# Layer 0's aggregation taken before its projection, its first loads in another order, and another order of the additions at the end of layer 1

## The chip, the cores and the metric

The kernel runs on one core of one Trainium2 chip. Its metric is the device time of one launch in microseconds. Five engines work side by side, each with an instruction queue of its own that is taken strictly in order: TensorE (PE, with its weight loads shown as PEld), VectorE (DVE), ScalarE (ACT), GpSimd (POOL) and the queue engine SyncE (SP). An instruction that waits holds back everything behind it on its engine, the DMAs that this engine issues among them.

## The reference, cut to what matters

There are 3327 tokens with 256 features, padded to 26 tiles of 128 tokens, and a dense adjacency of 3327 x 3327 numbers of which few are not zero. Each of two layers adds a graph aggregation and then a mixture of experts:

```python
# layer 0
x = x + relu(adj @ (layernorm(x) @ W) + b)
x = x + moe0(layernorm(x))                 # top 2 of 8 experts, hidden size 1024
# layer 1
x = x + relu(new_adj @ (tanh(layernorm(x) @ W_proj + b_proj) @ W_gcn) + b_gcn)
x = x + moe1(layernorm(x))                 # top 2 of 8 experts, hidden size 256
```

`new_adj` is tanh of the squared positive entries of `adj`, of which at most the 700 largest of each row are kept. No row has so many, so the kernel counts the positive entries and takes the branch without a selection.

## The kernel before, in words

The code is unrolled Python, and a scheduler fixes the order in each engine's queue when the kernel is built. Everything is 32-bit float; a matmul of 32-bit numbers is two records in the trace, and the counts of records below are those of the trace.

**Start of layer 0.** SP loads x tile by tile (L134), the weight W into `proj_sb` (L136), and then adjacency. The adjacency comes in 13 panels of 256 target nodes, each in two pieces of 13 source tiles (1664 KB each); a ring of six pieces in SBUF holds three panels. For each tile DVE computes the statistics (L267 to L279), PE turns the tile as it is, without normalising it (L305), ACT copies the result (L306), PE multiplies it by W (L313), and ACT writes the product, scaled by the tile's deviation, into `s` (L318). The mean is taken out of W itself once (L1053 to L1056). Ahead of all this 32 small matmuls on a constant keep PE busy (L144, `WARM`).

**Aggregation (`aggregate`, L345).** Both layers call it. For each panel the adjacency tile is the stationary operand and a tile of `s` the moving one, so that each of two PSUM sums holds 128 nodes by 256 features: 52 matmuls for a panel (L359). DVE adds bias, relu and x (`add_relu`, L323 and L324). Then `after0` routes the panel's two tiles: layernorm, 16 dot products with the gate (L379), the two best experts (`weights`, L436), an exponential on ACT (L444). One panel later `list_tokens` gives each token its row in an expert's list: four small matmuls on PE (L465, L466) and four scatters by POOL (L483). While this goes on ACT counts the positive entries of each piece with 16 sign activations a panel (`count`, L1069); a panel's piece of the ring is free when PE and ACT have both read it, and SP's load of the panel three further on waits for that (L341).

`after0(0)` also has SP turn two small gate weights through DRAM element by element (L1085), has POOL load the first of them onto all partitions (`load_gate`, L247), and has SP fill the first rows of all experts' lists (`fill`, L1035 and L1037, 32 DMAs).

**Experts (`experts`, L753).** The lists are worked in blocks of 256 tokens. A `step` loads blocks ahead, multiplies one (`first`, L873, activation L880), turns the next one (`turned`, L861 and L864) and multiplies on (`second`, L912); DVE adds the bias and scales (L919, L920), and POOL scatters the rows to DRAM (L483). After the first two steps of layer 0 the list of the last panel is made and the later blocks are planned.

**End of layer 1.** There are 32 steps, the last six of which work half blocks of 128 tokens. Beside the steps SP reads back the finished rows of pairs of tiles (`load_outputs`, L980), DVE adds them to x (`add_loaded`, L994), and ACT's queue stores the pair (L1329). In the branch that is taken a pair's additions come two steps after its read, inside the loop of steps. After the loop the last two pairs of tiles, which need every scatter, are read, added and stored (`finish`, L1287).

Of the kernel before, what the change touches and what calls it, by code (L numbers as in the profile page):

```python
# [10 lines left out]
F32 = mybir.dt.float32  # L11
# [11 lines left out]
P = 128  # L23
NT = 26
# [51 lines left out]


BEGUN, FIRST_TILES, MORE_TILES = 12, 14, 22
WARM = 32
TIERS = 3  # L80
# [10 lines left out]
def gnn_moe_two_layers(  # L91
# [38 lines left out]
    cum = state.tile([P, NT + 1, E], BF16, name="cum")  # L130

    proj_sb = const.tile([P, DC, D], F32, name="proj_sb")
    for t, n in [(0, 2)] + [(t, 4) for t in range(2, NT, 4)]:
        nc.sync.dma_start(out=x[:, t : t + n, :], in_=x_in[:, t : t + n, :])  # L134
        if t == 0:
            nc.sync.dma_start(out=proj_sb, in_=g0_w.rearrange("(c p) n -> p c n", p=P))  # L136


# [7 lines left out]
    make_identity(nc, ident)  # L146
    mean = ring[RING - 1][:, 0:P]
    nc.gpsimd.memset(mean, 1.0 / D)
    ones = const.tile([P, 1], F32, name="ones")
# [92 lines left out]

    f1_r_sb = by_feature("f1_r_sb", f1_rT)
    gates = []

    def load_gate(g):
# [4 lines left out]

    g1_bp_sb = plain("g1_bp_sb", g1_bp)
    f1_b1_sb = plain("f1_b1_sb", f1_b1)
    g1_wg_sb = by_feature("g1_wg_sb", g1_wg)

# [52 lines left out]

    def node_features(i, lhsT, w_sb, scale=None):

        ps = psy.tile([P, D], F32, name="ps_s", tag="py")
        for c in range(DC):
            nc.tensor.matmul(  # L313
                ps, lhsT=lhsT[:, c, :], rhs=w_sb[:, c, :], start=(c == 0), stop=(c == DC - 1)
            )
        if scale is None:
            return nc.scalar.copy(s[:, i, :], ps)
        return nc.scalar.activation(s[:, i, :], ps, AF.Copy, scale=scale)  # L318

# [10 lines left out]

    def piece(pan, k):
        return ring[(pan * NCHUNK + k) % RING].rearrange("p (c w) -> p c w", w=PW)

    last_piece, output_loads = [], []

    def load_panel(pan, prepare, earlier=()):

        for k in range(NCHUNK):
            a = piece(pan, k)
            with behind(earlier):  # L340
                d = nc.sync.dma_start(out=a, in_=adjT[pan, k])  # L341
            last_piece[:] = [d]
            prepare(pan, k, a)

    def aggregate(b_sb, prepare, after, loaded=0, count=None):  # L345

        for pan in range(NPAN):
# [3 lines left out]
            chunks = [piece(pan, k) for k in range(NCHUNK)]  # L351
            if count:
                count(pan, chunks)
            ps = [psy.tile([P, D], F32, name="ps_g", tag="py") for _ in range(PW // P)]
# [11 lines left out]
            for it in range(PW // P):  # L366
                add_relu(x[:, pan * (PW // P) + it, :], ps[it], b_sb)
            after(pan)

    def rows_of(a, t0, n):  # L370
# [382 lines left out]
    def experts(xlist, ys, group, fixed, n_hidden, func, w1T, b1, w2T, b2, copy, kept=None):  # L753
# [179 lines left out]

        def step(late, end=always, place=None):

            t = len(started)
            started.append(t)
            while len(loaded) < min(t + RING // places, end):
                load(late)
            if t not in ready:  # L940
                ready[t] = turned(loaded[t][1], groups_of(t))
            _, _, w1, bb1, _, _ = loaded[t]
            hT = first(ready.pop(t), w1, bb1, groups_of(t))
            if t + 1 < min(len(loaded), end):
                ready[t + 1] = turned(loaded[t + 1][1], groups_of(t + 1), place)
            second(t, late, hT)
# [68 lines left out]
    def fill(*lists):  # L1015


        with tc.issue_after(last_feature.ins):
            wide = blk.tile([P, H // P, SB], F32, name="wide").rearrange("p h b -> p (h b)")
# [12 lines left out]
            for xlist in lists:  # L1032
                for e in range(E):
                    first = xlist[e * NP : e * NP + SB, :].rearrange("(g p) d -> p g d", p=P)
                    nc.sync.dma_start(out=first[:, :, 0:ID], in_=zeros)  # L1035
                    with nc.allow_non_contiguous_dma("two elements of a partition"):
                        nc.sync.dma_start(  # L1037
                            out=first[:, :, ID : ID + 1], in_=rows_f[:, e, :].unsqueeze(2)
                        )

    deviation = {}
    for t0, n0 in [(0, 2), (2, 2), (4, 4), (8, 4), (12, 6), (18, 8)]:
        _, rs = statistics(t0, n0)
        deviation.update((t0 + g, rs[:, g : g + 1]) for g in range(n0))
        for t in range(t0, t0 + n0, 2):
            xT = turned_tiles([x[:, t + g, :] for g in range(2)])
            if t == 0:  # L1050
                ps = psy.tile([P, D], F32, name="ps_mean", tag="py")
                for c in range(DC):
                    nc.tensor.matmul(  # L1053
                        ps, lhsT=mean, rhs=proj_sb[:, c, :], start=(c == 0), stop=(c == DC - 1)
                    )
                nc.vector.tensor_tensor(  # L1056
                    proj_sb, proj_sb, ps.unsqueeze(1).to_broadcast([P, DC, D]), ALU.subtract
                )
            for g in range(2):
                last_feature = node_features(  # L1060
                    t + g, xT[:, :, ts(g, P)], proj_sb, deviation[t + g]
                )

    def count(pan, chunks):
        with tc.issue_after(last_feature.ins):
            for k, a in enumerate(chunks):
                for i in range(PW // GROUP):
                    sign = work.tile([P, CJ, GROUP], BF16, name="sign", bufs=1)
                    nc.scalar.activation(  # L1069
                        sign, a[:, :, ts(i, GROUP)], AF.Sign, bias=below,  # L1070
                        accum_out=positive[:, pan, i, k : k + 1],
                    )
# [6 lines left out]
    def after0(pan):  # L1079
        if pan == 0:  # L1080
            with tc.issue_after(last_piece[0].ins):
                for name, w in (("gate0", f0_wgT), ("gate1", f1_rT)):
                    g = dram.tile([E, D], F32, name=name)
                    with nc.allow_non_contiguous_dma("a few thousand elements"):
                        nc.sync.dma_start(out=g.rearrange("e d -> d e"), in_=w)  # L1085
                    gates.append(g)
            load_gate(gates[0])
            fill(xlist0, xlist1)
        if FREE_PAN <= pan < NPAN - 1:
            layer0.load(None)  # L1090
        t, n = PAIRS[pan]
        list_waiting()
        xn = layernorm(t, n)
# [6 lines left out]

    aggregate(gnn_b_sb, lambda pan, k, a: None, after0, count=count)

    layer0.step(None)
    layer0.step(None)
# [188 lines left out]
    with tc.If(first_usual > 0) as arms:  # L1293
# [28 lines left out]
        with tc.If(second_usual > 0) as inner:  # L1322
            layer1.know(2 * E)
            waiting, asked, added, k = [], [], [], 0
            while len(layer1.started) < layer1.always:
# [5 lines left out]
                if at == EARLY + 2 * E - 2:  # L1331
                    layer1.know_rest(late1)
                with behind(last_y):
                    if asked and at > asked[0][2] + 1:
                        yt, tiles, _ = asked.pop(0)
                        add_loaded(yt, *tiles)
                        added.append(tiles)
# [6 lines left out]
                if at in (EARLY + E, EARLY + 2 * E):  # L1344
                    tiles = range(0, FIRST_TILES, 2) if at == EARLY + E else range(FIRST_TILES, MORE_TILES, 2)
                    waiting.extend(((t, 2), at, list(outputs)) for t in tiles)
            assert not (waiting or asked)
            for tiles in added:
                nc.scalar.dma_start(out=rows_of(out, *tiles), in_=x[:, tiles[0] : sum(tiles), :])
            finish([(t, 2) for t in range(MORE_TILES, NT, 2)])  # L1350
        with inner.Else():
# [171 lines left out]
```

## Time and profile before

| What | Value |
|---|---|
| median of 3 runs | 1236.31 us (1234.97 to 1237.64) |
| the profiled execution's own time | 1235.14 us |
| its span | 1233.4 us, so 1.7 us lie around it |
| granted TensorE clock, mean | 0.99 |
| PE busy | 1198.3 us, 97% of the span |
| DVE, ACT, POOL busy | 698.1, 522.6, 271.7 us |
| DMA | 241.59 MB, mean 196 GB/s |

A line of the timeline gives the start in us, the length in us, the engine with the line of the kernel, the operation, what it writes and reads, how many instructions are merged in the line, and in brackets how long the engine had been idle and what released it. SPq, ACTq and POOLq are the parts of those engines that issue DMAs. Neighbouring lines of PE overlap a little, because matmuls are pipelined and their ends are modelled; distances between starts are what counts.

### The profile page before, as it was taken

How to read it: one execution, taken by the hardware profiler on the slowest of the kernel's cores; microseconds unless marked ns; L12 is line 12 of the kernel's file. 1: busy time of each engine (PE TensorE's matmuls, PEld its weight loads, DVE VectorE, ACT ScalarE, POOL GpSimd, SP SyncE). 2: the span in 40 equal slices, each digit the busy share in tenths (PEclk: the TensorE clock that was granted, in tenths of full speed). 3: DMA queues.
4: the chain of work that ended last, by engine and by line, in shares of the span. 5: the costliest groups of instructions: out<-in, count | busy, mean ns of one | idle time of the engine just before them, and what ended most of it. 6: DMA issues, size and time to landing. Idle time of an engine off the chain costs nothing. (4 is left out here: it accounts for less than half of the span.)

```text
span 1233.4 us, 18208 instructions
## 1 busy us (share of the span) xinstructions
PE 1198.3 (97%) x5853; PEld 1037.4 (84%) x5853; DVE 698.1 (57%) x2812; ACT 522.6 (42%) x963; POOL 271.7 (22%) x339
## 2 busy tenths in 40 slices
PE   8999999999999999999999999999999999999973
PEld 7888888888888888888888888888888888888862
DVE  6057877677664111211121167568999999786453
ACT  4869545541022222322222225896455453043331
POOL 2003131131231111111111110002323223255531
PEclk9999999999999999999999999999999999999996
DMA  9696455454167655766657657244445442477695
GB/s 349 187 241 246 176 201 176 147 191 142 63 233 231 208 195 175 240 201 204 233 179 229 224 223 268 79 167 172 164 177 195 161 158 90 128 245 248 209 288 195
DMA packets 122537, 241.59 MB, mean 196 GB/s; under 512 B 24352, under 2 KB 92992, under 8 KB 115392
## 3 DMA queue, kind: packets, MB, share of 16 engines
q1 hardware_dynamic: 107760, 205.33, 50.1%
q0 software_dynamic: 11136, 31.60, 7.0%
q10 hardware_dynamic: 3536, 3.41, 0.8%
q8 instruction: 48, 0.79, 0.3%
q14 instruction: 57, 0.47, 0.1%
HBM read 203.98 MB, written 36.33 MB: 195 GB/s over the span
## 5 line engine op out<-in xcount | busy, mean ns | idle before, releaser
L359 PE MATMUL ps_g<-s,ring 128*128 128x256 f32 x2704 | 588.2, 380 | 0.0
L359 PEld LDWEIGHTS ps_g<-s,ring 128*128 128x128 f32 x2704 | 512.0, 190 | 68.7
L873 PE MATMUL ps_h<-xT,ring 128*128 128x256 f32 (+1 forms) x1176 | 251.1, 366 | 3.3 <-ACT xT L864 2.1
L873 PEld LDWEIGHTS ps_h<-xT,ring 128*128 128x128 f32 x1176 | 205.6, 191 | 40.6 <-ACT wide L880 5.8
L880 ACT ACTIVATE wide<-ps_h,ring 128x256 f32<-128x256 f32 (+1 forms) x240 | 110.3, 460 | 283.9 <-PE ps_h L873 283.0
L379 DVE SCALAR_TENSOR_TENSOR rt_product<-xn,gate 128x256 f32<-128x256 f32 x400 | 198.0, 495 | 12.4
L912 PE MATMUL ps_y<-ring,wide 128*128 128x256 f32 x896 | 200.3, 379 | 0.0
L483 POOL DMA_INDIRECT xlist<-xn,rt_idx x104 | 106.4, 1023 | 398.6 <-DVE ln_ve L270 281.8
L912 PEld LDWEIGHTS ps_y<-ring,wide 128*128 128x128 f32 x896 | 167.1, 190 | 21.0
L1069 ACT ACTIVATE sign<-ring,below 128x416 bf16<-128x416 f32 x208 | 133.5, 642 | 66.4 <-DMA ring<-in_adjT 60.2
L483 POOL DMA_INDIRECT ys<-narrow,index x56 | 55.1, 985 | 330.9 <-DVE narrow L920 238.1
L1220 ACT ACTIVATE ring<-ring 128x3328 f32<-128x3328 f32 x22 | 65.4, 2979 | 87.2 <-DVE ring L1219 56.6
L864 DVE COPY xT<-ptb 128x512 f32<-128x512 f32 (+1 forms) x29 | 19.0, 654 | 147.0 <-PE ptb L861 147.0
L919 DVE TENSOR_TENSOR narrow<-ps_y,ring 128x256 f32<-128x256 f32 x56 | 23.8, 424 | 133.7 <-PE ps_y L912 130.7
L323 DVE TENSOR_TENSOR gnn_t<-ps_g,gnn_b_sb 128x256 f32<-128x256 f32 x52 | 21.9, 420 | 112.1 <-PE ps_g L359 99.0
L483 POOL DMA_INDIRECT ys<-wide,index x58 | 58.2, 1004 | 60.1 <-DVE wide L920 34.5
L1221 ACT ACTIVATE ring<-ring 128x3328 f32<-128x3328 f32 x22 | 65.4, 2977 | 0.6
L444 ACT ACTIVATE rt_d<-rt_d 128x2 f32<-128x2 f32 x26 | 5.3, 202 | 117.3 <-DVE rt_d L443 117.3
L912 PE MATMUL ps_y<-s,narrow 128*128 128x256 f32 (+1 forms) x200 | 49.3, 387 | 0.1
L267 DVE BATCH_NORM_STATS2 ln_st<-x 128x6 f32<-128x256 f32 x104 | 42.9, 419 | 4.0 <-DMA x<-in_x 2.9
L861 PE MATMUL ptb<-ident,ring 128*128 128x128 f32 x228 | 36.3, 279 | 5.3 <-ACT narrow L880 5.1
L1219 DVE TENSOR_SCALAR ring<-ring 128x3328 f32<-128x3328 f32 x22 | 41.3, 1883 | 0.0
(215 smaller groups left out, 964.2 us busy)
## 6 DMA issues: line engine op xcount, KB each, us to landing
ring<-in_adjT SPq DMA_DIRECT2D x52, 1664.0 KB, 7.6
ring<-in_f_w1T SPq DMA_DIRECT2D x30, 1024.0 KB, 6.2
ring<-in_f_w2T SPq DMA_DIRECT2D x30, 1024.0 KB, 8.1
ring<-xlist SPq DMA_DIRECT2D x52, 258.0 KB, 3.1
ring<-in_f_w SPq DMA_DIRECT2D x36, 256.0 KB, 3.6
ring<-ys SPq DMA_DIRECT2D x14, 512.0 KB, 4.2
ring<-in_f_b SPq DMA_DIRECT2D x34, 128.0 KB, 7.5
xlist<-wide SPq DMA_DIRECT2D x16, 257.0 KB, 6.3
```

What stands on the lines that cost most here:

```text
L267: nc.vector.bn_stats(out=st, in_=x[:, t0 + g, :])
L359: nc.tensor.matmul(ps[it], lhsT=chunks[k][:, c, ts(it, P)], rhs=s[:, j, :], start=(j == 0), stop=(j == NT - 1),)
L379: nc.vector.scalar_tensor_tensor(product, xn[:, g, 0, 0:D], 1.0, gate[:, e, :], ALU.mult, ALU.mult, accum_out=sc[:, g, e : e + 1],)
L483: d = nc.gpsimd.indirect_dma_start(out=a[:, :], out_offset=bass.IndirectOffsetOnAxis(ap=index, axis=0), in_=rows_, in_offset=None,)
L861: nc.tensor.transpose(pt[:, c, ts(g, P)], xb[:, g, ts(c, P)], ident)
L873: nc.tensor.matmul(ps, lhsT=w1[:, c, ts(hc, P)], rhs=xT[:, c, :], start=(c == 0), stop=(c == DC - 1),)
L880: nc.scalar.activation(hT[:, hc, :], ps, func, bias=bb1[:, hc : hc + 1])
L912: last_product[:] = [nc.tensor.matmul(ps, lhsT=hT[:, hc, ts(g, P)], rhs=w2[:, hc, :], start=(hc == 0), stop=(hc == hc_n - 1),)]
L1069: nc.scalar.activation(sign, a[:, :, ts(i, GROUP)], AF.Sign, bias=below, accum_out=positive[:, pan, i, k : k + 1],)
L1219: nc.vector.tensor_scalar(a, a, 0.0, None, ALU.max)
L1220: nc.scalar.activation(a, a, AF.Square)
L1221: nc.scalar.activation(a, a, AF.Tanh)
```

## The change

**Layer 0 aggregates the normalised tokens.** `aggregate_first` takes the place of `aggregate` in layer 0 (layer 1 keeps it). DVE writes the normalised tiles straight into `s`. A tile of `s` is the stationary operand now and the adjacency the moving one, so that a panel's two sums hold 128 features by 256 nodes: 52 matmuls as before. ACT copies the two sums out, and four matmuls a panel (`finish`, 8 records) multiply by W behind the panel: six source tiles into the next panel (`BEHIND`), and for the last panel inside the first step of the experts. The first two panels are worked source tile by source tile side by side for the first 13 tiles; after that each panel by itself. The turning of x, the copies of it and the product with the mean are gone. The constant matmuls ahead are 54 instead of 32.

**Loads.** x and the first pieces of panels 0 and 1 are loaded in five groups of tiles in turn, W after the second pieces of these panels. The first gate is turned ahead of panel 2's pieces, the second behind them. The lists are filled in two halves, at panels 1 and 4. Four small weights are loaded later. The list of panel 0 is made a panel later.

**End of layer 1.** In the last six steps no additions are made any more: four pairs of tiles wait until behind DVE's last output. The last four tiles are read, added and stored one by one, and two of these stores go by SP's queue.

```diff
-WARM = 32
+WARM = 54
+BEHIND = 5
...
-    for t, n in [(0, 2)] + [(t, 4) for t in range(2, NT, 4)]:
+    for t, n in [(0, 2), (2, 2), (4, 4), (8, CJ - 8), (CJ, NT - CJ)]:
         nc.sync.dma_start(out=x[:, t : t + n, :], in_=x_in[:, t : t + n, :])
-        if t == 0:
-            nc.sync.dma_start(out=proj_sb, in_=g0_w.rearrange("(c p) n -> p c n", p=P))
+        if t < CJ:
+            for pan in range(2):
+                nc.sync.dma_start(
+                    out=piece(pan, 0)[:, t : t + n, :], in_=adjT[pan, 0, :, t : t + n, :]
+                )
...
+    def aggregate_first(b_sb, w, w_sb, begin, count, after):
+        sums, waiting, copied = {}, [], []
+        def start(pan):
+            sums[pan] = [psy.tile([P, PW], F32, name="ps_g", tag="py") for _ in range(DC)]
+        def add(pan, j):
+            for c in range(DC):
+                nc.tensor.matmul(
+                    sums[pan][c], lhsT=s[:, j, ts(c, P)],
+                    rhs=piece(pan, j // CJ)[:, j % CJ, :],
+                    start=(j == 0), stop=(j == NT - 1),
+                )
+        def finish():
+            pan, g = waiting.pop()
+            for it in range(PW // P):
+                ps = psh.tile([P, D], F32, name="ps_o", tag="ph")
+                for c in range(DC):
+                    nc.tensor.matmul(
+                        ps, lhsT=g[:, c, ts(it, P)], rhs=w_sb[:, c, :], start=(c == 0),
+                        stop=(c == DC - 1),
+                    )
+                add_relu(x[:, pan * (PW // P) + it, :], ps, b_sb)
+            after(pan)
+        def rest(pan, first):
+            for j in range(first, NT):
+                add(pan, j)
+                if waiting and j == first + BEHIND:
+                    finish()
+            g = work.tile([P, DC, PW], F32, name="xnT", bufs=2)
+            for c in range(DC):
+                copied.append(nc.scalar.copy(g[:, c, :], sums[pan][c]))
+            waiting.append((pan, g))
+        loaded = RING // NCHUNK
+        for pan in range(loaded):
+            load_panel(pan, lambda pan, k, a: None, begun=1 if pan < 2 else 0)
+            if pan == 1:
+                nc.sync.dma_start(out=w_sb, in_=w.rearrange("(c p) n -> p c n", p=P))
+                with tc.issue_after(last_piece[0].ins):
+                    turn_gate(f0_wgT)
+        with tc.issue_after(last_piece[0].ins):
+            turn_gate(f1_rT)
...
+        for j in range(CJ):
+            for pan in range(2):
+                add(pan, j)
+        for pan in range(NPAN):
...
+            begin(pan)
+            count(pan, copied)
+            rest(pan, CJ if pan < 2 else 0)
+        return finish
...
     for t0, n0 in [(0, 2), (2, 2), (4, 4), (8, 4), (12, 6), (18, 8)]:
-        _, rs = statistics(t0, n0)
...
+        with behind(last_normalized if t0 < 12 else ()):
+            layernorm(t0, n0, xn=s[:, t0 : t0 + n0, :].unsqueeze(2))
...
-    aggregate(gnn_b_sb, lambda pan, k, a: None, after0, count=count)
-
-    layer0.step(None)
+    def begin(pan):
+        if pan in (1, 4):
+            fill(xlist0 if pan == 1 else xlist1)
+
+    finish_last = aggregate_first(gnn_b_sb, g0_w, proj_sb, begin, count, after0)
+
+    layer0.step(None, between=finish_last)
     layer0.step(None)
...
                 with behind(last_y):
-                    if asked and at > asked[0][2] + 1:
+                    if asked and asked[0][2] + 1 < at <= layer1.always - FIXED[1]:
                         yt, tiles, _ = asked.pop(0)
                         add_loaded(yt, *tiles)
                         added.append(tiles)
...
-            for tiles in added:
-                nc.scalar.dma_start(out=rows_of(out, *tiles), in_=x[:, tiles[0] : sum(tiles), :])
-            finish([(t, 2) for t in range(MORE_TILES, NT, 2)])
+            left = []
+            for i, t in enumerate(range(MORE_TILES, NT)):
+                yt = ring[i][:, 0 : K * D].rearrange("p (n d) -> p n d", n=1)
+                load_outputs(yt, ys1, t, 1, outputs)
+                left.append((yt, (t, 1)))
+            with behind(last_y):
+                for i, (yt, tiles) in enumerate([(yt, tiles) for yt, tiles, _ in asked] + left):
+                    add_loaded(yt, *tiles)
+                    queue = nc.sync if i > len(asked) and i % 2 else nc.scalar
+                    queue.dma_start(out=rows_of(out, *tiles), in_=x[:, tiles[0] : sum(tiles), :])
```

## The prediction

> **What bounds the kernel now.** I read the page first (PE busy 97% of the span, clock 0.99), then who waits on PE, then the timelines of the two places that the change touches. PE waits for others for some 14 us in all, so time is won by taking work off PE or by letting it start earlier, and behind PE's last matmul by shortening the end. PE's timeline at the start:
>
> ```profile
> 4.57 2.04 PE L1053 MATMUL ps_mean<-proj_sb,ring 128*128 128x256 f32 x4
> 14.76 3.72 PE L313 MATMUL ps_s<-proj_sb,xnT 128*128 128x256 f32 x16 [2.30 <-ACT xnT L306]
> ...
> 41.03 45.06 PE L359 MATMUL ps_g<-s,ring 128*128 128x256 f32 x208
> ```
>
> Aggregation begins at 41.03, behind the whole projection. From 41.03 to the next group at 85.92 are 208 records, so a record is 0.216 us, a matmul 0.43, a panel 22.5. At 335.41 the first step of the experts begins.
>
> DVE's timeline gives the price of a layernorm, at the start and in panel 0:
>
> ```profile
> 3.79 0.75 DVE L267 BATCH_NORM_STATS2 ln_st<-x 128x6 f32<-128x256 f32 x2 [2.62 <-DMA x<-in_x]
> ...
> 65.27 0.17 DVE L270 TENSOR_SCALAR ln_ve<-ln_mv 128x2 f32<-128x2 f32 x1
> ...
> 67.72 0.73 DVE L289 TENSOR_SCALAR xn<-x,ln_mv,ln_guess 128x256 f32<-128x256 f32 x2
> ```
>
> The chain of small operations between statistics and normalising takes 2.45 us (65.27 to 67.72) however many tiles share it, a tile's normalising 0.37.
>
> The DMA view of the first 60 us, GB/s in slices of 1.5 us:
>
> ```profile
> GB/s 0 162 255 246 360 345 144 357 403 419 431 431 419 408 426 426 426 426 426 426 426 426 426 426 435 365 119 1 0 1 1 4 12 23 24 94 135 239 310 351
> ```
>
> By 12 us 2.8 MB have come, then 0.42 MB a us. At the end, DVE's timeline and the chain that ended last:
>
> ```profile
> 1213.78 0.42 DVE L919 TENSOR_TENSOR wide<-ps_y,gate 128x256 f32<-128x256 f32 x1
> 1215.31 0.69 DVE L994 TENSOR_TENSOR x<-x,ring 128x512 f32<-128x512 f32 x1 [1.05 <-DMA ring<-ys]
> 1215.92 0.35 DVE L920 TENSOR_SCALAR wide<-wide,ring 128x256 f32<-128x256 f32 x1
> 1227.70 1.42 DVE L994 TENSOR_TENSOR x<-x,ring 128x512 f32<-128x512 f32 x2 [0.16 <-DMA ring<-ys]
> ```
>
> ```profile
> 1216.55 5.59 DMA ys<-wide,index
> ...
> 1223.12 4.50 DMA ring<-ys
> ```
>
> PE's last product ends near 1213.1, yet the last output is scaled only at 1215.92: an addition that waits 1.05 us for its read stands in between. The last scatter (1216.55), the last read and the additions follow one another.
>
> **Start, the gain.** PE's time before 41.03 disappears: projection, turning, its waits. In its place PE starts when two tiles are normalised: statistics at 3.79 as now, small operations from 4.80, normalising from 7.25, so the first matmul at 7.6 instead of 41.03. The 54 constant matmuls, at 3.6 us for 32 (L144), end near 7.2 and cost nothing.
>
> **Start, what PE still waits for.** A source tile feeds both panels with 8 records, 1.73 us. DVE works groups of 2, 2, 4, 4, 6 and 8 tiles, the first four strictly one after another: 0.37 + 0.15 a tile for statistics, 2.45 for the chain, then 0.37 a tile. So tile 2 is ready at 11.8, tile 4 at 16.8, tile 8 at 22.5; in the last two groups statistics and small operations interleave as they do now from 11 to 20 us, so tile 12 comes at 31 to 32.5. PE has used up two tiles at 11.1, four at 15.3, twelve at 30.6: it waits 0.7, 1.5 and 0.4 to 1.9, 2.6 to 4.1 in all. I take 3.4, bounds 2 (if DVE interleaves better) and 7 (each group 1 us later). The present wait of 2.30 at 14.76 left the clock at full, so none of these should cost clock.
>
> **Start, loads.** Each source tile brings 3 x 131 KB, and PE uses them at 227 GB/s. The first 13 tiles are 5.1 MB, here at 17.5 us by the curve above, and used until 32; the second pieces come at 26 to 30 and are needed at 34 and 46. DVE, not DMA, sets the pace, so I price the splitting at nothing; without that cover it costs whatever a piece is late. The row for small transfers: the first 256 KB of x landed in 3.0 us, with slices of 162 to 360 GB/s. The Trainium skill speaks against the split ("DMA: Bandwidth & Descriptors", table of measured bandwidth): batch to 1 MiB or more for three quarters of the peak, and at 64 KB about a third. By a third of 420 GB/s the 5.1 MB would take 36 us and PE would lose some 7 more; the slices of this trace are already above that rate, and I stay with them.
>
> **Panels.** 52 matmuls of the same shape as before, with the operands' roles exchanged: 22.5 us, unchanged. Added on PE: 8 records a panel, 13 x 1.73 = 22.4 us. These are the 104 records of L313 moved, no longer at the start but behind each panel. Start in sum: 41.03 - 7.6 - 3.4 - 22.4 = 7.6 us gained, bounds 4.0 and 9.0.
>
> **What hides the rest.** ACT copies two sums a panel (0.47 each by L318) behind 16 signs (0.77 apart, 12.3 us of a panel of 24.3). The built order of ACT puts the exponential of panel p-1 ahead of panel p's copies, so routing must not lag: DVE's chain from bias to exponential takes 15.0 (63.67 to 78.70) to 16.9 us with a list in it, starts 6 us into the next panel, and is over at 23 of 24.3. The PE queue needs the copies only 5.2 us into the panel after; 5 us of cover. Behind that wait would stand all matmuls of the panel, and DVE's routing waits for them. Moved steps: the 16 fills ahead of panel 4's loads on SP took some 19 us (32 took 41.2 to 78.6), and panel 4 is needed past 107; the four small weights, and POOL's gate load, have only constants or later lists behind them; W for layer 1 now waits on POOL until the last panel's product, hundreds of us before its use. Block 0 of the experts was loaded at 277 and turned at 312: 5 to 7 us later is still early. In the first step the last panel's product (already counted) puts its routing 8 us later; the list stands behind the second step, some 5 us after routing ends. All nothing, as long as these covers hold.
>
> **End.** The stall of PE from 1197 to 1201 stays: that addition belongs to step 26, which the new condition still allows. In the half-block steps PE is paced by its own chain with ACT, not by the additions. Without them DVE scales the last output right behind its sum, at 1213.6 instead of 1215.92, and the scatter starts at 1214.2. Its landing took 2.4 to 5.6 us in these last 40 us; I take 3.9: 1218.1. SP needed 1.0 us from there to the second read's issue, 1.9 for four: the fourth goes out at 1220.0, lands after 3.5 to 4.5 (3.6 taken, half the bytes), 1223.6; two additions of one tile 0.9: 1224.5, against 1229.12. The four pairs put off take 4 x 1.42 = 5.7 us of DVE from 1214 and are over by then. Gain 4.6; with all long ends and the four tiles queued on DVE 2.0, with all short ones 6.3. I take 4.5; stores behind the last addition are priced as now.
>
> **Sum.** 7.6 + 4.5 = 12.1 off the profiled execution's 1235.14 (span 1233.4 and 1.7 around it): 1223.0. That execution lies 1.2 below the median of 1236.31, so I forecast 1224.2.
>
> **Rivals.** *Slower: the element-wise turning holds up panel 2.* SP's timeline:
>
> ```profile
> 15.70 0.68 SPq L1085 DMA_DIRECT2D gate<-in_f_wgT  x1
> 17.38 23.72 SPq L1085 DMA_DIRECT2D gate<-in_f_rT  x1
> ```
>
> The second turning kept SP's queue 23.72 us, the first landed after 32.9. The first now stands ahead of panel 2's pieces, the second ahead of panel 3's. If pieces wait for the whole landing: 20 + 32.9 + 17.5 (median landing of a piece in the first 60 us) = 70 against a need at 58.8, 11.6 us of PE; the second gives some 9 more, and after the gap of 4.1 us at 1197 PE ran at clock 0.50 for 3 us, so 3 more: 1247. It decides once panel 2 lands more than 12 us late. Against it: data ahead of the first turning are 10.5 MB, gone at 30; in the trace the bytes stop at 39 and the turning has landed at 48.6, so it takes 9 us by itself, and panel 2 lands at 48. 7%.
>
> *Hand-over late, gain gone.* If routing takes 6 us more than its 17, each panel's copies and product come late, about 1 us a panel: 11 us, 1235. For it: four engines pass each panel on. Against: DVE is busy 17.8 of 23 us in its fullest panel, and panels have become longer. 8%.
>
> *The end gives nothing*, because reads, stores and scatters share a busy DMA there (share 0.9 at 1217 to 1220) and only the order changes: 1228.7. 9%.
>
> **How the numbers follow.** The forecast has 76%. Its bounds are 6.0 and 15.3 of gain, 1220 to 1230 from both bases; with the third rival and some noise the range is 1219 to 1231, and the two others are left out. A measurement here tells 0.2%, 2.5 us, from no change. Faster by more: 76 + 9 + 2 of the second rival, 0.87; same 0.04; slower 7 + 2, 0.09.
>
> **What would show it.** Right: the first aggregation matmul at 7 to 9 us, 2 to 7 us of waits on PE before 36, panels 24.3 apart, the first expert step near 327 (335.41 now), no wait at the product behind a panel, last scaling within 1 us of PE's last product, last addition about 4.5 us sooner after that product than now. Wrong: panel 2's first matmul waiting for DMA, a wait for ACT at each product, or a first matmul past 12 us.

## The result, and the profile after

The changed kernel took **1223.68 us** (median of 4 runs, 1222.62 to 1224.82) where the kernel before took 1235.89 us (4 runs, 1234.97 to 1237.64) beside it: ratio 0.9904, 95% interval 0.989 to 0.9919, so 12.2 us less. The profiled execution took 1222.76 us with a span of 1221.0; its PE is busy 1188.4 us, again 97%.

PE's timeline of the changed kernel (start, length, what; in brackets the idle time and its releaser):

```profile
7.69 3.72 PE L383 MATMUL ps_g<-ring,s 128*128 128x256 f32 x16 [0.92 <-DVE s L297]
13.63 3.72 PE L383 MATMUL ps_g<-ring,s 128*128 128x256 f32 x16 [2.22 <-DVE s L297]
18.45 14.08 PE L383 MATMUL ps_g<-ring,s 128*128 128x256 f32 x64 [1.10 <-DVE s L297]
33.05 18.40 PE L383 MATMUL ps_g<-ring,s 128*128 128x256 f32 x84 [0.52 <-DVE s L297]
...
65.96 22.61 PE L383 MATMUL ps_g<-ring,s 128*128 128x256 f32 x104
88.41 1.89 PE L396 MATMUL ps_o<-proj_sb,xnT 128*128 128x256 f32 x8
90.34 22.69 PE L383 MATMUL ps_g<-ring,s 128*128 128x256 f32 x104
```

Aggregation begins at 7.69 instead of 41.03 and waits 2.22 + 1.10 + 0.52 = 3.84 us between tiles. Panels start 24.38 apart (65.96 to 90.34). The product stands behind a panel without a bracket: nobody is waited for. The first expert step begins at 327.35 (335.41 before).

DVE's timeline and the DMA view (GB/s in slices of 1.5 us, 0 to 60 us) tell what the waits consist of:

```profile
9.78 0.76 DVE L275 BATCH_NORM_STATS2 ln_st<-x 128x6 f32<-128x256 f32 x2 [1.83 <-DMA x<-in_x]
...
26.31 0.75 DVE L275 BATCH_NORM_STATS2 ln_st<-x 128x6 f32<-128x256 f32 x2 [1.23 <-DMA x<-in_x]
```

```profile
GB/s 0 182 317 105 223 217 289 415 334 394 412 420 431 441 428 408 435 426 426 426 376 164 22 0 80 71 71 390 412 417 418 418 442 254 20 0 80 76 35 177
```

DVE itself waits for x, 1.83 us for tiles 2 and 3 and 1.23 us later. By 12 us 2.62 MB have come (2.80 before), and from 33 to 40 us little moves: there the loads stand behind the element-wise turning in SP's queue.

At the end, the timeline of all engines around the half blocks (the last six steps, of 128 tokens), then DVE's last work:

```profile
1189.46 0.69 DVE L1064 TENSOR_TENSOR x<-x,ring 128x512 f32<-128x512 f32 x1 [2.34 <-DMA ring<-ys]
...
1191.39 0.63 ACT L948 ACTIVATE narrow<-ps_h,ring 128x128 f32<-128x128 f32 x2 [3.60 <-DVE wide L987]
...
1191.81 0.44 PE L929 MATMUL ptb<-ident,ring 128*128 128x128 f32 x2 [2.72 <-ACT narrow L948]
```

```profile
1202.46 0.35 DVE L988 TENSOR_SCALAR wide<-wide,ring 128x256 f32<-128x256 f32 x1
1202.73 2.49 DVE L1064 TENSOR_TENSOR x<-x,ring 128x512 f32<-128x512 f32 x4
...
1215.47 0.89 DVE L1064 TENSOR_TENSOR x<-x,ring 128x256 f32<-128x256 f32 x2 [0.49 <-DMA ring<-ys]
```

The addition of step 26 waits 2.34 us for its read and PE stands 2.72 us behind it (4.11 before). The last scaling now follows PE's last product (start 1200.83) after 1.63 us instead of 3.96, with the additions behind it. The chain that ended last:

```profile
1203.09 4.76 DMA ys<-wide,index
...
1209.72 5.66 DMA ring<-ys
```

The last read takes 5.66 us though it is half as large as before (4.50). From the last scaling to the end of the span it is 18.5 us (17.5 before): behind the last scaling the new end has lost a microsecond.

### The profile page after: what moved, and what is told of

The parts are those of the page before. It is cut to its first block, busy times and chain, and to the rows that moved or that the text cites. A ratio compares the mean times of both kernels' runs of the same rounds, so it can differ in the third digit from the quotient of the medians.

```text
span 1221.0 us, 18156 instructions
## 1 busy us (share of the span) xinstructions
PE 1188.4 (97%) x5819; PEld 1029.2 (84%) x5819; DVE 706.9 (58%) x2841; ACT 512.0 (42%) x950; POOL 270.5 (22%) x341
## 5 line engine op out<-in xcount | busy, mean ns | idle before, releaser
L383 PE MATMUL ps_g<-ring,s 128*128 128x256 f32 x1352 | 295.6, 380 | 4.8 <-DVE s L297 4.8
L360 PE MATMUL ps_g<-s,ring 128*128 128x256 f32 x1352 | 294.2, 380 | 0.0
L383 PEld LDWEIGHTS ps_g<-ring,s 128*128 128x128 f32 x1352 | 255.7, 190 | 40.3 <-DVE s L297 6.1
L360 PEld LDWEIGHTS ps_g<-s,ring 128*128 128x128 f32 x1352 | 256.0, 190 | 34.4
L447 DVE SCALAR_TENSOR_TENSOR rt_product<-xn,gate 128x256 f32<-128x256 f32 x400 | 198.6, 496 | 12.2
L329 DVE TENSOR_TENSOR gnn_t<-ps_o,gnn_b_sb 128x256 f32<-128x256 f32 x26 | 11.0, 424 | 82.5 <-PE ps_o L396 82.5
```

The source lines that it names most:

```text
L360: nc.tensor.matmul(ps[it], lhsT=chunks[k][:, c, ts(it, P)], rhs=s[:, j, :], start=(j == 0), stop=(j == NT - 1),)
L383: nc.tensor.matmul(sums[pan][c], lhsT=s[:, j, ts(c, P)], rhs=piece(pan, j // CJ)[:, j % CJ, :], start=(j == 0), stop=(j == NT - 1),)
L447: nc.vector.scalar_tensor_tensor(product, xn[:, g, 0, 0:D], 1.0, gate[:, e, :], ALU.mult, ALU.mult, accum_out=sc[:, g, e : e + 1],)
```

## The experiments

They ran in three groups, each on one chip with the kernel before beside it: e1 to e4 (kernel before 1246.11 us), e5 to e8 (1235.5), e9 to e12 (1242.95). Times are compared inside a group, or as ratios to the kernel before.

The theory to be tested: start and end are independent; the start gives some 7.5 us, the end 4 to 5, but the end's gain comes from other places than forecast. The rivals stand with each run. The following table, from the starts in each trace, carries most readings. "Half blocks begin" is the start of the first half block's matmul on PE. The three last columns are stretches that follow one another: from that start to the start of PE's last product, from there to the start of the last scaling, and from there to the end of the span.

| Kernel | first expert step | half blocks begin | PE's wait in them | to last product | to last scaling | to the end |
|---|---|---|---|---|---|---|
| before | 335.41 | 1194.01 | 4.11 | 17.95 | 3.96 | 17.48 |
| before, again (e9) | 335.45 | 1202.65 | 2.95 + 1.59 | 16.82 | 4.21 | 17.82 |
| new start, old end (e1) | 327.15 | 1198.71 | 2.69 | 16.48 | 3.98 | 17.43 |
| old start, new end (e2) | 337.92 | 1204.66 | 2.67 | 16.35 | 1.62 | 17.57 |
| changed | 327.35 | 1185.77 | 2.72 | 15.06 | 1.63 | 18.54 |
| changed, again (e5) | 327.34 | 1185.94 | 1.76 | 14.10 | 1.63 | 18.13 |
| both gates first (e6) | 327.18 | 1188.02 | 2.17 | 15.90 | 1.63 | 18.45 |
| product sooner (e7) | 326.91 | 1185.51 | 2.79 | 15.13 | 1.63 | 18.33 |
| x ahead (e8) | 326.53 | 1187.22 | 2.00 | 14.35 | 1.62 | 18.11 |
| last tiles in pairs (e3) | 327.17 | 1198.91 | 2.24 | 14.58 | 1.63 | 18.98 |
| no stores of the pairs (e10) | 326.98 | 1196.45 | 2.27 | 15.98 | 1.64 | 16.73 |
| step 26 put off (e4) | 327.22 | 1198.51 | 0 | 12.41 | 1.63 | 18.95 |
| step 26 put off, x between (e11) | 326.20 | 1198.39 | 0.16 + 0.43 | 12.87 | 1.63 | 18.71 |
| all additions later, x between (e12) | 325.67 | 1192.58 | 0 | 12.40 | 1.63 | 19.79 |

### The two halves alone: e1, e2

e1 is the changed kernel with the old condition and the old code behind the loop; e2 is the kernel before with the new ones:

```diff
# e1 (e2 the other way round; the code behind the loop is left out here)
-                    if asked and asked[0][2] + 1 < at <= layer1.always - FIXED[1]:
+                    if asked and at > asked[0][2] + 1:
```

> Layer 0's new start with the old end of layer 1 (additions inside the loop, last four tiles in two pairs). The prediction's split says 7.6 us under the kernel before, that is some 4.6 over the changed kernel, with the same stall of PE of about 4 us and the same half clock near the end. The rival from the two traces: the stall of PE before the half blocks was 2.72 us in the changed kernel and 4.11 before, and the clock stayed full behind it; if this came with the new start (everything is merely shifted in time against the reads), the start alone gives 7.5 + 3 = 10 to 11 us, and the end little.

> The old start with the new end of layer 1. The prediction's split says 4.5 us under the kernel before, all of it behind the last scaling and by the additions taken out of the way. The rival from the two traces: 2.3 us from the additions out of the way, about 1 us lost again behind the last scaling by four reads of one tile instead of two of two, so 1.3 us; 4.5 or more only if the shorter stall and the full clock (some 3 us) belong to the new end.

The start alone: 1238.72 us, ratio 0.993 (0.9908 to 0.9953), by the ratio 8.7 us less than the kernel before, 5.9 to 11.5 (the medians differ by 7.4). The end alone: 1241.81 us, ratio 0.9962 (0.9948 to 0.9976), 4.7 us less, 3.0 to 6.5 (medians 4.3). The sum, 13.4, agrees within these intervals with the 12.2 of the whole change: the halves add up, and both sizes of the prediction, 7.6 and 4.5, lie inside the intervals. e2's rival falls, since the end alone is worth more than 1.3 us. e1's rival, 10 to 11 us, is still inside e1's interval by time; against it speaks the trace, where the way through the half blocks is as long with the new start (16.48 us) as with the new end (16.35), so the new start does not carry the difference there. On this chip the old start itself was slower in the trace of e2 (first aggregation at 43.53, 41.03 in the kernel before), which is why 8.7 may be a little much for the start.

The old end seen alone, on DVE in e1:

```profile
1218.56 0.69 DVE L1064 TENSOR_TENSOR x<-x,ring 128x512 f32<-128x512 f32 x1 [1.71 <-DMA ring<-ys]
1219.17 0.35 DVE L988 TENSOR_SCALAR wide<-wide,ring 128x256 f32<-128x256 f32 x1
```

An addition that waits for its read stands ahead of the last scaling, as in the kernel before. In the table the way from last product to last scaling is 3.96 to 4.21 with the old end and 1.62 to 1.64 with the new, in every trace: 2.4 us belong to the additions taken out of the way.

### How far one trace can be trusted: e5, e9

> The changed kernel as it is, as the measure for the runs beside it on the same chip: 0.990 of the kernel before. In its trace the stall of PE ahead of the half blocks is looked at once more: 2.2 to 4.1 us if it hangs on when one read lands; always 2.7 if it belongs to the new order.

> The kernel before, traced once more. In its first trace PE stood 4.11 us ahead of the half blocks and ran at half clock behind it; in the runs with the new start or the new end the same stall was 1.8 to 2.8 us. If the length hangs on when one read lands, this trace shows another length (2 to 4 us) and, if it is under 3, less or no half clock, so the 3.6 us by which the changed kernel's half blocks came out shorter than before are for the most part a difference of two executions. If the old order itself makes it longer, it is 4 us again.

The changed kernel again: 1224.34 us, ratio 0.9906 (0.9886 to 0.9926). The kernel before again, one run, 1243.36 us. The wait of PE in the half blocks was 1.76 and 2.95 us here, 2.72 and 4.11 in the first traces, so it hangs on when one read lands. Nevertheless the old end is longer in all three traces that have it. From the half blocks to the last product it takes 17.95, 16.82 and 16.48 (mean 17.08), the new end with its four pairs and single tiles 16.35, 15.06, 14.10, 15.90, 15.13 and 14.35 (mean 15.15). The mean difference is 1.9 us, not the 2.9 of the first pair of traces. Its parts are worked out below.

### The stall itself: e4

```diff
-                    if asked and asked[0][2] + 1 < at <= layer1.always - FIXED[1]:
+                    if asked and asked[0][2] + 1 < at < layer1.always - FIXED[1]:
```

> The changed kernel with a strict condition, so that the addition of step 26 is put off as well (five pairs wait behind the last output instead of four). Theory: this addition waits 2.34 us for its read on DVE, holds the index and the output of the step behind it, and so makes the wait of 2.72 us on PE; without it PE's wait is 0 to 0.5 and the kernel 2 to 2.7 us faster; the fifth pair's additions, 1.4 us, lie in the 6 us in which DVE waits for the last scatter. Rival: PE's wait hangs on the block's other inputs (index, rows, weights): it stays above 2 us and the time within 0.5 us of the changed kernel.

1232.97 us, ratio 0.9888 (0.987 to 0.9907). PE's timeline, where the stall was:

```profile
1198.51 1.05 PE L941 MATMUL ps_h<-xT,ring 128*128 128x128 f32 x8
...
1201.89 0.44 PE L929 MATMUL ptb<-ident,ring 128*128 128x128 f32 x2
```

No bracket where the stall was. The half blocks take 12.41 us to the last product instead of 15.06 in the changed kernel, 2.65 less: the theory's number, and the other inputs of the block are not what PE waits for. The changed kernel did not run in this group, so its time is compared by ratio: 0.9888 against 0.9904 (0.9906 in e5) is some 2 us less, with intervals that overlap. That the stall is gone is shown by the trace; that the kernel is faster by it is likely, not shown.

### The last four tiles: e3, e10

e3 reads, adds and stores the last four tiles in two pairs; e10 leaves the stores of the four pairs that were put off out:

```diff
# e3
-            for i, t in enumerate(range(MORE_TILES, NT)):
-                yt = ring[i][:, 0 : K * D].rearrange("p (n d) -> p n d", n=1)
-                load_outputs(yt, ys1, t, 1, outputs)
+            for i, t in enumerate(range(MORE_TILES, NT, 2)):
+                yt = ring[i][:, 0 : 2 * K * D].rearrange("p (n d) -> p n d", n=2)
+                load_outputs(yt, ys1, t, 2, outputs)
...
# e10
-                    queue.dma_start(out=rows_of(out, *tiles), in_=x[:, tiles[0] : sum(tiles), :])
+                    if i >= len(asked): queue.dma_start(out=rows_of(out, *tiles), in_=x[:, tiles[0] : sum(tiles), :])
```

> The changed kernel, but the last four tiles are read, added and stored in two pairs, all stores by ACT's queue; the additions still stand behind the last output. The prediction counted on the single tiles for most of 2 us (last addition earlier by landing of half the bytes and 0.9 for the last two additions instead of 1.42): by that this run is 1 to 2 us slower than the changed kernel. The rival: four small reads landed in 5.7 us in the changed kernel against 4.5 for the pairs before, so single tiles cost as much as they bring: within 0.5 us, or up to 1 us faster with pairs.

> The changed kernel without the stores of the four pairs that were put off (their rows of the output stay unwritten); their additions are made as before. Behind the last scaling the six runs with the new end took 17.6 to 19.0 us to the end, the old end 17.4, and the forecast 15. Theory: the stores of the pairs (256 KB each) share the DMA engines with the last scatter and the four last reads, which landed in 4.8 and 5.7 us instead of 3.9 and 3.6; without them the tail is 1.5 to 2.5 us shorter (16 to 17). Rival: reads and scatter are as slow by themselves, the tail stays within 0.5 us of 18.3.

e3: 1236.81 us, ratio 0.9924 (0.9902 to 0.9946); its way from last scaling to the end is 18.98, against 18.19 as the mean of the six traces with single tiles (17.57 to 18.54). Single tiles bring 0.8 us by this one trace, less than the 1 to 2 us counted on; by ratio e3 is some 2.5 us slower than the changed kernel (0.9924 against 0.9904), with intervals that overlap. e10: 1234.38 us, ratio 0.9934 (0.991 to 0.9959); from last scaling to the end 16.73, below all six. Its chain that ended last:

```profile
1214.69 4.59 DMA ys<-wide,index
...
1220.31 3.99 DMA ring<-ys
```

The read in this chain is the third of the four, and it lands in 3.99 us without the stores. With four pairs' stores the third took 4.77 (e5) and 4.79 (e7), and where the chain goes by the fourth, that took 4.28 to 5.66. From the scatter's landing to the end of the last addition it is 6.80 us in e10 and 7.68 to 8.51 in the six kernels with these stores. The scatter is as slow as with them (4.59 against 4.43 to 4.76). So the stores beside the last reads cost some 1.3 to 1.5 us of the tail, by one trace without them; the theory held for the reads, not for the scatter. (As a whole e10 is not faster than the changed kernel, 0.9934 against 0.9904 with intervals that overlap: its half blocks took 15.98 us with a stretch at half clock, and one wait for `xT` ahead of them was 4.73 us.)

### The start: e6, e7, e8

```diff
# e6
                     turn_gate(f0_wgT)
+                    turn_gate(f1_rT)
-        with tc.issue_after(last_piece[0].ins):
-            turn_gate(f1_rT)
# e7
-BEHIND = 5
+BEHIND = 1
# e8: x one group ahead of its pieces
-    for t, n in [(0, 2), (2, 2), (4, 4), (8, CJ - 8), (CJ, NT - CJ)]:
-        nc.sync.dma_start(out=x[:, t : t + n, :], in_=x_in[:, t : t + n, :])
+    for t, n, xs in [(0, 2, [(0, 2), (2, 2)]), (2, 2, [(4, 4)]), (4, 4, [(8, CJ - 8)]), (8, CJ - 8, [(CJ, NT - CJ)])]:
+        for a, m in xs: nc.sync.dma_start(out=x[:, a : a + m, :], in_=x_in[:, a : a + m, :])
```

> The changed kernel with the second gate's turning moved ahead of panel 2's pieces too. In the changed kernel the first turning held SP's queue from 17.7 to 35.2 and panel 2's bytes came between 39 and 48, with 12 us to spare. Theory (the prediction's rival of the turning, and where it decides): a second turning in the same place holds the queue some 9 to 17 us more, panel 2 lands at 57 to 67 where PE needs it at 60: 0 to 8 us slower than the changed kernel, with a wait for DMA ahead of panel 2's first matmuls if it is over 60. Rival: the held time is not additive, the two turnings run side by side on the queues and panel 2 still lands near 50: no difference beyond 1 us.

> The changed kernel with the product of a panel two source tiles into the next panel (1.7 us behind the panel's last matmul) instead of six (5.2 us). In the changed kernel ACT copied the two sums 0.3 us behind the last matmul and was done 1.2 us after it, so 4 us of the 5.2 are spare. By that: no wait of PE at the product, time within 1 us of the changed kernel. Rival: in some panels the exponential of routing or the signs stand ahead of the copies, which the five tiles cover; then PE waits 1 to 3 us in these panels, 5 to 20 us in all.

> The changed kernel with each group of x loaded one group ahead of the pieces that it works with (x of tiles 2 and 3 second in the queue, and so on). Theory: what PE waits for at the start is in part DMA and not DVE alone: DVE waited 1.83 us for x of tiles 2 and 3 and 1.23 us for x behind tile 13. With x ahead tile 2 is ready at 11.7 instead of 13.5, PE's waits up to 36 fall from 4.8 to about 3 us, and the kernel is 1.5 to 2 us faster. Rival (the prediction's claim that DVE alone sets the pace): the waits of PE stay above 4 us and the time within 0.5 us; or pieces come late now, and PE waits for DMA instead.

e6: 1224.0 us, ratio 0.9903 (0.9885 to 0.9921): no difference. SP's timeline of the changed kernel, then of e6:

```profile
17.73 17.50 SPq L344 DMA_DIRECT2D ring<-in_adjT  x2
35.27 0.55 SPq L143 DMA_DIRECT2D gate<-in_f_rT  x1
35.96 17.21 SPq L344 DMA_DIRECT2D ring<-in_adjT  x2
```

```profile
17.61 16.99 SPq L143 DMA_DIRECT2D gate<-in_f_rT  x1
34.65 13.63 SPq L344 DMA_DIRECT2D ring<-in_adjT  x4
```

The hold on the queue is real: whatever stands behind the first turning gets through only 17.0 us later (17.02 us of the first line are panel 2's first piece). The 17.21 us of the third line are something else: panel 3's pieces wait there for ACT's signs to free the ring (16.8 us by the waits on SP). A second turning in the same place adds little to the hold: panel 2's first piece is through SP at 38.25 in e6 instead of 34.75, 3.5 us later. The stretch with hardly any bytes is longer, to 46 instead of 40 us. Added up from the slices, the 3.4 MB of panel 2 are there near 49 in the changed kernel and near 55 in e6 (estimates), and PE comes to them at 59; the second piece landed at 56.0 and 60.8, where PE needs it at 72. So some 5 to 6 us of cover went, and no time.

e7: 1223.86 us, ratio 0.9905 (0.9886 to 0.9925): no difference either. PE's timeline:

```profile
47.39 1.89 PE L396 MATMUL ps_o<-proj_sb,xnT 128*128 128x256 f32 x8
```

Even two tiles behind the panel nobody waits at the product, so of the 5.2 us of cover that the prediction counted, 3.5 were to spare.

e8: 1223.51 us, ratio 0.9901 (0.9877 to 0.9925), in time not told apart from the changed kernel. PE's timeline, then two of its windows (length, PE busy with records, granted clock, DMA share, GB/s):

```profile
8.57 42.06 PE L383 MATMUL ps_g<-ring,s 128*128 128x256 f32 x180 [2.76 <-DMA ring<-in_adjT]
```

```profile
8.00:10.00 2.00, 1.43 (x4) 0.50 0.94 278
12.00:14.00 2.00, 2.00 (x6) 0.50 1.04 351
```

All waits for DVE between the tiles are gone, 3.84 us, but not only because x comes sooner. The first piece comes later, PE waits 2.76 us for it, starts at 8.57, and then runs at half clock until some way past 14 us (0.85 from 14 to 16); the changed kernel was granted 1.00 there. The 180 records take 41.90 us to the next product, where 180 x 0.216 are 38.9: 3 us are lost to the clock. DVE did get ahead as the theory says: it begins to normalise tile 12 at 30.99 instead of 32.59. The first expert step begins 0.8 us earlier. So the claim that DVE alone sets the pace falls, since DVE itself waits for x, and the clock can account for the 0.7 to 1.2 us that are missing from the expected 1.5 to 2. Two runs below load x nearly as early. e12, at full clock there, begins the first expert step 1.7 us before the changed kernel; e11, at clock 0.53 and 0.62 from 10 to 14 us, 1.15.

### A version that goes further: e11, e12

```diff
# both: x between the two pieces of the group before
+    def load_x(t, n): nc.sync.dma_start(out=x[:, t : t + n, :], in_=x_in[:, t : t + n, :])
+    load_x(0, 2)
+    for t, n, t1, n1 in [(0, 2, 2, 2), (2, 2, 4, 4), (4, 4, 8, CJ - 8), (8, CJ - 8, CJ, NT - CJ)]:
+        for pan in range(2):
+            nc.sync.dma_start(out=piece(pan, 0)[:, t : t + n, :], in_=adjT[pan, 0, :, t : t + n, :])
+            if pan == 0:
+                load_x(t1, n1)
# e11, in the loop of steps
+                    if asked and asked[0][2] + 1 < at < layer1.always - FIXED[1]:
# e12, in the loop of steps
+                    if asked and asked[0][2] + 2 < at < layer1.always - FIXED[1]:
```

> The changed kernel with the addition of step 26 put off as well, and x loaded between the two pieces of the group before (x of tiles 2 and 3 third in the queue instead of fourth). By the runs before: PE's stall ahead of the half blocks gone (1.8 to 2.8 us), the tail 0.4 longer by the fifth pair, the first expert step 0.5 to 1 us earlier because DVE does not wait for x of tiles 2 and 3 and the first pieces are not pushed back as with x fully ahead (where PE waited 2.76 us for its first piece and began at 8.57). Together 2 to 3.5 us under the changed kernel. Against it: the additions put off pile up behind the last scatter, and the tail gives it back.

> As the run before, and each addition of a pair three steps behind its read instead of two (six pairs wait behind the last output). Theory: the waits of PE for ACT's xT in the last full blocks (1.7 us and more at steps ahead of the half blocks) come from additions that hold DVE until their read lands, as at step 26; one step later the read is there, these waits fall from 3 us to under 1, and the kernel is 1 to 2 us faster than the run before. Rival: the read lands late because its issue waits for scatters, whose step it follows anyway; then the waits stay, and six pairs (8.5 us of additions) make the tail longer: the same or up to 1 us slower.

e11: 1230.42 us, ratio 0.9897 (0.9876 to 0.9919). Against the changed kernel's 0.9904 that is 0.9 us, inside both intervals: the 2 to 3.5 us expected are not shown. Its trace has the stall gone and the start 1.15 us ahead, but a wait of 4.07 us for `xT` ahead of the half blocks. e12: 1228.16 us, ratio 0.988 (0.9856 to 0.9903), the shortest time relative to the kernel before of all runs. Against the changed kernel by ratio it is some 3 us less and against e11 2.3 us, both with intervals that overlap; that it is faster is likely, not shown. (e10, the nearest kernel on this chip, took 6.2 us more than e12, but e10 had itself a longer time by ratio than the changed kernel.) In e12's trace the way from half blocks to last product is 12.40, as in e4, and in PE's timeline from 1160 us on the only wait is one of 1.69 us that the profile puts down to no other engine. DVE's additions wait for no read between 1050 us and the half blocks' end, where in e11 they wait 6.7 us, 4.5 of them ahead of the wait for `xT`: what the theory says. The price is behind the last scaling:

```profile
1212.54 6.99 DMA ring<-ys
```

With six pairs' stores beside it the last read takes 6.99 us, and the tail 19.79 us, the longest.

## Why the prediction was right or wrong, point by point

**Start.** The first matmul (7.6, measured 7.69), the distance of panels (24.3, measured 24.38), the cost of the exchanged operands (none: 380 ns a record on average in both layers), the product (8 records, 1.89 us on PE) and the first expert step (near 327, measured 327.35) are as forecast, the last by some luck: by the prediction's own terms it is 335.41 - 7.6 - 1.73 = 326.1. One step failed: "DVE, not DMA, sets the pace, so I price the splitting at nothing". It rested on the bytes of the kernel before's curve, and on the first 256 KB of x, which landed in 3.0 us. The 256 KB pieces of the changed kernel's start landed after 5.6 us (median), x of tiles 2 and 3 reached DVE at 9.78 where DVE was free at 7.95, and each later group is late with it. PE's waits, 3.4 forecast, are 3.84 by the brackets; by the distances of starts they are 33.05 - 7.69 less 96 records of 0.216 us, 4.6 us. So the mis-sized term is PE's wait, 3.4 taken and 4.6 measured, most of it ahead of tile 2 (0.7 forecast, 2.22 by the bracket), whose x is fourth in SP's queue. (A slip adds 0.3: by the prediction's own prices tile 4 is ready at 17.1, not 16.8.) It is the order of the loads that e8 and e12 show to matter, with the pieces split just the same; what the splitting as such costs no run here shows. The prediction's estimate by the Trainium skill ("DMA: Bandwidth & Descriptors", table of measured bandwidth), which took the share of the table's 64 KB row for pieces of 256 KB and more, was 7 us; the slices here, 105 to 415 GB/s up to 12 us with several pieces under way at once, lie for the most part well above a third of 420.

With that term the start is 41.03 - 7.69 - 4.6 - 22.4 = 6.3 us, and in the second expert product the changed kernel is 6.26 us ahead (336.58 against 342.84). At layer 1's first aggregation it is 7.4 us ahead (782.54 against 789.98; e10 against e9 7.85). The missing 1.1 us is a wait in the second step of the kernel before, which the changed kernel does not have and the prediction did not count:

```profile
352.57 5.45 PE L873 MATMUL ps_h<-xT,ring 128*128 128x256 f32 x24 [0.94 <-ACT wide L880]
```

The kernel before has it again in e9; e5 and e10 do not have it. Why it is gone was not examined.

**Covers.** All were there. The element-wise turning (the slower rival) holds SP's queue for 17.0 us, longer than the 9 that were reckoned for it, and still panel 2 came some 10 us ahead of its need (an estimate from the slices); e6 took about half of that away without a loss. The late hand-over has no trace at all: no wait at any product, not even with `BEHIND` at 1.

**End.** The total was right (4.5 forecast, 4.7 alone, 3.0 to 6.5), its parts were not:
- additions out of the way: forecast 2.3, measured 2.3 (3.96 to 1.63), and the same in every pair of traces;
- behind the last scaling: forecast 10.9 us to the end of the last addition and 2.2 us gained, measured 13.90 and 0.7 lost, 1.1 by the end of the span (the mean of six traces against the three of the old end: 18.19 against 17.58 to the end, 0.6 lost). The mis-sized terms are the scatter's landing (3.9 taken, 4.76 measured) and the last read's (3.6 taken for half the bytes, 5.66 measured). The prediction let the four pairs' additions lie in DVE's gap but not their four stores in the gap of the DMA; only its third rival named the shared DMA. Without the stores the way from the scatter's landing to the last addition is 0.9 to 1.7 us shorter (e10);
- half blocks: forecast unchanged ("The stall of PE from 1197 to 1201 stays"), measured 1.9 us shorter on average. The stall did stay, for the reason named (e4), but its length differs from run to run. The claim beside it, that PE in the half blocks is paced "not by the additions", does not hold in every execution of the old end. In e9 an addition inside the half blocks waits for its read, and PE's last product waits behind it:

```profile
1216.89 0.69 DVE L994 TENSOR_TENSOR x<-x,ring 128x512 f32<-128x512 f32 x1 [1.70 <-DMA ring<-ys]
```

```profile
1219.47 1.13 PE L912 MATMUL ps_y<-s,narrow 128*128 x4 [1.59 <-ACT narrow L880]
```

The sign "last addition about 4.5 us sooner after that product than now" failed as well: from the start of PE's last product to the end of the last addition it is 15.53 us, 17.16 before, 1.6 sooner.

The sum over these means, 2.4 + 1.9 - 0.6 = 3.7 us, agrees with the time of e2. Two errors of about 2 to 3 us with opposite signs cancelled: the total of the end was right by luck. The 1.9 us of the half blocks can be taken apart. Less PE's waits, the way to the last product is 12.3 to 12.4 us in nine traces of the table and 13.7 to 13.8 in the five that have half clock there. So 1.4 of the 1.9 us are shorter waits (0.5 of them the one of e9), and 0.5 is the clock. Whether the first stall is shorter because of the new end is not settled, nor is the clock: two of three traces with the old end have a stretch at half clock there and three of the eight with the stall and the new end (e2, e6, e10), and that is too little to tell a cause from chance.

## What to carry to other kernels

An operation that waits for a DMA and stands in an engine's queue ahead of work that others need can cost its whole wait (2.34 us on DVE, 2.72 on PE here); put behind the last such work it no longer did, and two steps between a read and its use were not enough here (e4). What is put off brings its stores with it: price them on the DMA beside the transfers that end last, not only its arithmetic on the engine. And when a stage's gain agrees with the forecast, check the terms; here the total of the end agreed with two of its three terms wrong. When a reordering removes one wait, look at the clock behind the wait that takes its place (e8).

## What the runs showed of the hardware that was not expected

**Half clock after short gaps.** The windows of PE behind the stall, e6 and then e7 (length, PE busy, granted clock, DMA share, GB/s):

```profile
1194.00:1196.00 2.00, 2.00 (x10) 0.61 0.90 284
1196.00:1198.00 2.00, 2.00 (x9) 0.54 0.71 240
```

```profile
1193.00:1195.00 2.00, 1.94 (x14) 1.00 0.87 273
```

e6 ran at half clock for some 3 us after a gap of 2.17 us, e7 at full clock after one of 2.79. Ahead of the half blocks' second turning, gaps of 2.17, 2.27, 2.67, 2.69 and 4.11 us were followed by half clock, gaps of 1.76, 2.00, 2.24, 2.72, 2.79 and 2.95 were not; at the start, gaps of 2.76 (e8) and 1.47 (e11, with one of 0.58 shortly ahead of it) were, the one of 2.22 in the changed kernel was not. In this range the length does not decide, so the prediction's inference from one gap of 2.30 that such waits cost no clock was not safe. The Trainium skill ("TensorE: Matmul & The Clock Gate", Part 1) puts half clock behind an idle window of about 3.4 us that runs freely; that the phase matters would fit, but six gaps shorter than that window led to half clock here, and the measurement decides.

**A queue behind element-wise DMA.** 2048 single elements (8 KB) held the next DMA of SP's queue for 17.0 us in the changed kernel and in e6, whether it was a panel's piece or a second turning, for 19.2 in e8, and for 23.7 in the kernel before. Two of them did not hold it twice: in e6 the piece behind both was held 3.6 us more.
